# Turning half of a decoder's attention probabilities in 32 by 32 blocks on VectorE, with transfers within SBUF in place of TensorE transposes

## The chip, the cores and the metric

The kernel runs on one core of a Trainium2 chip. The metric is the device time of one execution in microseconds; a time of several runs is their median. TensorE, VectorE, ScalarE and GpSimd each work through their own instructions strictly in order, and so does SyncE, which here only issues transfers (DMA). An instruction that has to wait for another engine or for a transfer holds up everything behind it on its own engine. In views of the profile PE is TensorE, PEld its weight loads, DVE is VectorE, ACT is ScalarE, POOL is GpSimd, SP or SPq is SyncE.

## The reference

One decoder layer over 8 batch elements of 512 tokens with 256 channels, all in float32. Three blocks follow each other, each with a residual and a layer norm: a linear attention with its own MLP, a softmax cross-attention to a context of 512 tokens with 128 channels, and a feed-forward stage that picks one of 8 adapters for each batch element. The change touches the cross-attention alone, which is this:

```python
def _L0_xattn_ref(q, kv, Wq, Wk, Wv, Wo, bo):
    NUM_HEADS = 16
    HEAD_DIM = 64
    ...
    scores = jnp.einsum('bhnd,bhmd->bhnm', qh, kh) * scale
    attn = jax.nn.softmax(scores, axis=-1)
    out = jnp.einsum('bhnm,bhmd->bhnd', attn, vh)
    out = out.transpose(0, 2, 1, 3).reshape(B, N, INNER)
    return out @ Wo + bo
...
x = _layernorm(x + _L0_xattn_ref(x, ctx_512, ...), axis=-1)
```

There are 16 heads of 64 channels, 512 queries and 512 keys. For each batch element and head the probabilities are a 512 by 512 matrix.

## The kernel before

**How the work is cut.** A batch element's 512 tokens are NT = 4 chunks of 128. The cross-attention takes two heads together, a *pair*, so there are NPAIR = 8 pairs; one head's 64 channels lie on partitions 0 to 63 and the other's on 64 to 127. For each pair `cross_attention` projects queries, keys and values (`qT`, `kT`, `v2`), and then goes through two *halves* of two chunks each. For each chunk `soft` (from L764) does the following, with the two heads' work side by side:

1. TensorE makes the scores of 128 queries against 512 keys, for both heads, into one of two PSUM tiles of the room `sc` (L770).
2. VectorE takes the negated maximum over the keys (L777).
3. ScalarE takes the exponential into a tile `p`, one for each head, 128 queries on the partitions by 512 keys, and sums on the way (L785).
4. VectorE takes the reciprocal of the sums (L790).
5. GpSimd scales `p` by it (L796), or ScalarE does (L794).
6. TensorE turns `p` in four transposes of 128 by 128 into a PSUM bank (L806), since the weighing needs keys on the partitions.
7. ScalarE (L328), or VectorE (L330), copies the bank into the half's tile `pT` of that head.

When both chunks of a half have come so far, `weigh` multiplies `v2` by the two `pT` tiles in 16 matrix multiplications (L825), and the result is copied into `oT`. After each fourth pair `project_out` multiplies by `Wo` (L841). A `pT` tile holds 4 blocks of 128 keys by 256 queries; the columns of the result in `oT` are these 256 queries in order.

**Rooms.** Tiles come from named rooms with a fixed number of places. `p` has 8 places, `x` (a whole batch element's tokens) 5, `pT` 2 and two more that it shares with `prod`, the products of the linear attention (L515, L538). PSUM has 4 banks and 2 score tiles.

**What sets the order.** Nothing on the compute engines is ordered by hand. Each piece of work is given to `task` with its engine, its length in nanoseconds, a due time, what it reads and what it writes. Work with `others` can go to a second engine. `play` then steps through a model of time: whenever an engine is free, it takes the piece with the earliest due time whose inputs are ready and whose tiles have room. The instructions of each engine are written out in the order found, and that order is fixed from then on. A `slack` is added to the time at which a piece's results count as ready; for transfers it stands for the landing. Due times are in units of PACE = 3,200 ns, 64 of them for a batch element. The linear attention and the MLP of later batch elements, and the feed-forward stage of the one before, run between the pieces of the cross-attention.

**Transfers.** All are issued by SyncE: inputs and weights at the start, then for each batch element one load of `x` (L432), one of the context (L702), and one store of the result (L962; four for the last one, L956). Each transfer signals on one of 8 semaphores in turn.

Of the kernel before, what the change touches and what calls it, by code (L numbers as in the profile page):

```python
# [18 lines left out]
P = 128  # L19
B, S, C = 8, 512, 256  # L20
NT = S // P
# [8 lines left out]
NPAIR = H2 // 2  # L30
# [20 lines left out]
PACE = 3200.0  # L51

WINDOWS = {0: (-200, -136), 1: (-8, 34), 2: (34, 84), 3: (84, 136)}


@with_exitstack
def decoder(ctx: ExitStack, tc: tile.TileContext, t: dict, out: bass.AP):
# [29 lines left out]
    def room(name, n, shape, pool=const):  # L87
        rooms[name] = [[pool.tile(shape, F32, name=f"{name}_{i}"), 0.0] for i in range(n)]
# [90 lines left out]

    room("bank", 4, [P, 512], psum)  # L180
    room("sc", 2, [P, 2, S], psum)
    room("x", 5, [P, NT, C])
    room("xhat", 1, [P, NT, C])
    room("xnT", 1, [P, KC, S])
    room("y1", 1, [P, NT, C])
# [15 lines left out]
    room("qT", 1, [P, S])  # L201
    room("kT", 1, [P, S])
    room("v2", 2, [P, NT, P])
    room("p", 8, [P, S])

    room("pT", 2, [P, NT * 2 * P])
    rooms["pT"] += rooms["prod"][2:]
    room("oT", 5, [P, S])
    room("bu", 1, [P, C])
# [116 lines left out]
    def copy(e, dst, src):  # L326
        if e == "act":
            nc.scalar.copy(dst, src)  # L328
        else:
            nc.vector.tensor_copy(dst, src)  # L330
# [363 lines left out]
    def cross_attention(b, begin):  # L694
        x, x1T, ctx = xs[b], Val("x1T"), Val("ctx")
        P8 = 8 * PACE

        def when(pr, step):
            return begin + (8 * pr + step) * PACE

        task(
            "sp", 0, begin - 60000, lambda: nc.sync.dma_start(out=ctx.t, in_=t["ctxT"][b]), (), [(ctx, 0)], slack=4000  # L702
        )
        turn(x1T, x, when(0, -12))
        for c in range(NT):
            task(
                "pool", 730, when(0, 2 + c),
                lambda e, c=c: add(e, x.t[:, c, :], x.t[:, c, :], bo2),
                [(x, c)], [(x, c)], ("bo2",), others=[("dve", 420, 4000)],
            )  # L710
        goes = []
        out_norm = Norm(x)
        oTs = []
        for pr in range(NPAIR):
            cols = slice(pr * P, (pr + 1) * P)
            qT, kT, v2, oT = Val("qT"), Val("kT"), Val("v2"), Val("oT")
            oTs.append(oT)
            ps_q, ps_k, ps_v = Val("bank"), Val("bank"), Val("bank")

            def project_q(ps=ps_q, cols=cols):  # L720
                for kc in range(KC):
                    nc.tensor.matmul(ps.t, Wq[:, kc, cols], x1T.t[:, kc, :], start=kc == 0, stop=kc == KC - 1)  # L722

            def project_v(ps=ps_v, cols=cols):
                for m in range(NT):
                    keys = slice(m * P, (m + 1) * P)
                    nc.tensor.matmul(ps.t[:, keys], ctx.t[:, keys], Wv[:, 0, cols], start=True, stop=True)  # L727

            task("pe", mm(512, 2), when(pr, -9), project_q, chunks(x1T), [(ps_q, 0)], ("Wq",), "full", holds=[qT])
            task("act", 600, when(pr, -8.8), lambda ps=ps_q, qT=qT: nc.scalar.mul(qT.t, ps.t, D2**-0.5), [(ps_q, 0)], [(qT, 0)])  # L730
            task(
                "pe", mm(512, 1), when(pr, -8),
                lambda ps=ps_k, cols=cols: nc.tensor.matmul(ps.t, Wk[:, 0, cols], ctx.t, start=True, stop=True),
                [(ctx, 0)], [(ps_k, 0)], ("Wk",), "full", holds=[kT],
            )
            task(
                "act", 590, when(pr, -7.8), lambda e, ps=ps_k, kT=kT: copy(e, kT.t, ps.t), [(ps_k, 0)], [(kT, 0)],
                others=[("dve", 690, 1500)],
            )
            task("pe", mm(128, 4), when(pr, -3), project_v, [(ctx, 0)], [(ps_v, 0)], ("Wv",), "full", holds=[v2])  # L740
            task(
                "act", 600, when(pr, -2.5),
                lambda e, ps=ps_v, v2=v2: copy(e, v2.t.rearrange("p m d -> p (m d)"), ps.t), [(ps_v, 0)], [(v2, 0)],
                others=[("dve", 690, 1500)],
            )
            for half in range(2):
                pT = [Val("pT"), Val("pT")]
                for c in (2 * half, 2 * half + 1):
                    soft(qT, kT, pT, c, when(pr, 4 * half - 6) + 0.1 * (c % 2) * PACE, when(pr, 2 * c))
                weigh(v2, pT, oT, half, when(pr, 4 * half + 6))  # L750
            if pr % 4 == 3:
                for c in range(NT):
                    project_out(x, oTs[pr - 3 :], range(pr - 3, pr + 1), c, when(pr, (13, 15, 16, 17)[c]))
                    if pr == NPAIR - 1:
                        out_norm.stats(c, when(pr, 18))
        out_norm.scale(range(NT), when(NPAIR, 11))
        for c in range(NT):
            out_norm.put(x, c, when(NPAIR, 11) + c, "dve")

    def halves(pT):  # L760
        return pT.t[:, : NT * 2 * P].rearrange("p (m n) -> p m n", m=NT)


    def soft(qT, kT, pT, c, due, turn_due):  # L764
        ps, nmax, ssum, rinv = Val("sc"), Val("nmax"), Val("ssum"), Val("rinv")

        def scores():
            for i in range(2):
                rows = slice(i * D2, (i + 1) * D2)
                nc.tensor.matmul(  # L770
                    ps.t[:, i, :], qT.t[rows, c * P : (c + 1) * P], kT.t[rows, :], start=True, stop=True
                )

        task("pe", mm(512, 1), due, scores, [(qT, 0), (kT, 0)], [(ps, 0)], kind="rows")
        task(
            "dve", 1217, due + 0.2 * PACE,
            lambda: nc.vector.tensor_reduce(nmax.t, ps.t, AX.X, ALU.max, negate=True), [(ps, 0)], [(nmax, 0)],  # L777
        )
        ps_ = []
        for i in range(2):  # L780
            p = Val("p")
            ps_.append(p)
            task(
                "act", 788, due + (0.5 + 0.2 * i) * PACE,
                lambda i=i, p=p: nc.scalar.activation(  # L785
                    p.t, ps.t[:, i, :], AF.Exp, bias=nmax.t[:, i : i + 1], accum_out=ssum.t[:, i : i + 1]
                ),
                [(ps, 0), (nmax, 0)], [(p, 0), (ssum, i)], kind="exp",
            )
        task("dve", 158, due + 0.8 * PACE, lambda: nc.vector.reciprocal(rinv.t, ssum.t), [(ssum, 0), (ssum, 1)], [(rinv, 0)])  # L790
        for i, p in enumerate(ps_):
            def scale(e, i=i, p=p):
                if e == "act":
                    nc.scalar.mul(p.t, p.t, rinv.t[:, i : i + 1])  # L794
                else:
                    nc.gpsimd.tensor_scalar(p.t, p.t, rinv.t[:, i : i + 1], 1.0, ALU.mult, ALU.mult)  # L796

            task(
                "pool", 715, due + (1 + 0.2 * i) * PACE, scale, [(p, 0), (rinv, 0)], [(p, 0)],
                others=[("act", 631, 1200)],  # L800
            )
            bank = Val("bank")

            def transpose(p=p, bank=bank):
                for m in range(NT):
                    nc.tensor.transpose(bank.t[:, m * P : (m + 1) * P], p.t[:, m * P : (m + 1) * P], ident)  # L806

            task("pe", 436, turn_due + i * PACE, transpose, [(p, 0)], [(bank, 0)], kind="full", holds=[pT[i]])
            task(
                "act", 587, turn_due + (i + 0.2) * PACE,  # L810
                lambda e, i=i, bank=bank: copy(
                    e, halves(pT[i])[:, :, (c % 2) * P : (c % 2 + 1) * P], bank.t.rearrange("p (m n) -> p m n", m=NT)
                ),
                [(bank, 0)], [(pT[i], c % 2)], others=[("dve", 690, 1000)],
            )


    def weigh(v2, pT, oT, half, due):
        av = Val("bank")

        def emit():
            for m in range(NT):
                for i in range(2):
                    cols = slice(i * D2, (i + 1) * D2)
                    nc.tensor.matmul(  # L825
                        av.t[cols, : 2 * P], v2.t[:, m, cols], halves(pT[i])[:, m, :], start=m == 0, stop=m == NT - 1
                    )

        task("pe", 1728, due, emit, [(v2, 0)] + [(pT[i], j) for i in range(2) for j in range(2)], [(av, 0)], kind="cols", holds=[oT])
        def put(e):  # L830
            to, of = oT.t[:, half * 2 * P : (half + 1) * 2 * P], av.t[:, : 2 * P]
            copy(e, to, of)

        task("act", 370, due + 0.5 * PACE, put, [(av, 0)], [(oT, half)], others=[("dve", 424, 100)])
# [255 lines left out]
```

## Time and profile before

| | |
|---|---|
| Median of 3 runs | 1831.79 us (1829.74 to 1832.67) |
| Profiled execution, its own time | 1831.43 us |
| Its span, first to last instruction | 1829.7 us |
| Instructions | 24,550 |
| Mean granted TensorE clock | 0.969 |
| TensorE transposes of `p` (L806) | 2048, busy 291.5 us |
| Copies of the turned `p` on ScalarE | 404, 594 ns each |
| Copies of the turned `p` on VectorE | 108, 677 ns each |
| Transfers by SyncE, all sizes | 3.3% of 16 engines' span |

The profile is one execution. Its page gives the busy time of each engine, the span in 40 slices with a digit for each engine's busy tenths, and rows for groups of instructions: line, engine, operation, what it writes and reads, shapes and count, then busy microseconds and the mean nanoseconds of one, then the idle time of the engine just before them and whose end it waited for. A view of a stretch gives for each engine its busy time with the number of instructions, then the granted clock of TensorE, the share of the transfer engines, and GB/s. A view in order of time gives start, length, engine, line, operation and tiles. A view of transfers gives the count, the size of one and the median time from issue to landing. Matrix multiplications overlap each other, so the mean length of one is more than its share of TensorE's time; the distance from one start to the next is that share.

### The profile page before, as it was taken

The page shows a single profiled execution, that of the slowest core. Times are in us where ns is not written, and L with a number is a line of the kernel's source. Part 1 is how long each engine was busy: PE and PEld are TensorE (multiplying, and loading weights), DVE is VectorE, ACT ScalarE, POOL GpSimd, SP SyncE. Part 2 cuts the span into 40 slices and gives each one's busy share as a digit, 9 for nine tenths or more (in the row PEclk, how much of TensorE's full clock was granted, in tenths as well). Part 3 has the DMA queues.
Part 4 walks back from the last instruction along what each step waited for, and adds up shares of the span by engine and source line. Part 5 has one row for each costly group of instructions (what it writes and reads, how often), then busy time and mean ns, then how long its engine had stood idle before and what let it go on. Part 6 is the DMA issues. An engine that isn't in the chain of part 4 may idle for free.

```text
span 1829.7 us, 24550 instructions
## 1 busy us (share of the span) xinstructions
PE 1678.7 (92%) x8720; PEld 1025.2 (56%) x8720; DVE 1326.5 (72%) x2141; ACT 1117.0 (61%) x2423; POOL 1078.1 (59%) x913
## 2 busy tenths in 40 slices
PE   3638999999999989999999999999999999999996
PEld 1534556555656545665556655666556655665662
DVE  8998987887868787779758887769758444555444
ACT  0205756667756677667665776667666667556643
POOL 6557775787676764767537864588537321343432
PEclk7769999999999999999999999999999999999998
DMA  8000000000000000000000000000000000000000
GB/s 256 1 1 1 1 1 1 7 1 1 1 7 29 1 1 1 7 30 1 1 1 12 24 1 1 1 24 1 1 1 12 13 1 1 7 12 1 7 13 17
DMA packets 18458, 22.70 MB, mean 12 GB/s; under 512 B 2720, under 2 KB 15648, under 8 KB 18336
## 3 DMA queue, kind: packets, MB, share of 16 engines
q1 hardware_dynamic: 16928, 19.03, 3.3%
q0 software_dynamic: 1408, 2.10, 0.5%
q8 instruction: 69, 1.13, 0.3%
q14 instruction: 53, 0.43, 0.1%
HBM read 16.93 MB, written 4.19 MB: 12 GB/s over the span
## 4 chain that ended last, share of the span: by engine, by line
PE 59%; DVE 20%; POOL 4%; ACT 4%; issue 3%; DMA 0%; POOLq 0%; ACTq 0%; DVEq 0%
PE bank L825 10%; PE sc L770 9%; PE bank L806 9%; PE bank L841 5%; PE bank L618 4%; PE bank L722 4%; DVE nmax L777 4%; DVE kv L524 3%; PE bank L643 3%; DVE o L547 3%; PE bank L467 3%; PE bank L869 2%; PE bank L972 2%; PE bank L727 2%; ACT p L785 2%
## 5 line engine op out<-in xcount | busy, mean ns | idle before, releaser
L796 POOL TENSOR_SCALAR p<-p,rinv 128x512 f32<-128x512 f32 x392 | 280.5, 729 | 400.5 <-DVE rinv L790 335.5
L785 ACT ACTIVATE p<-sc,nmax 128x512 f32<-128x512 f32 x512 | 348.7, 689 | 142.4 <-DVE nmax L777 113.2
L777 DVE TENSOR_REDUCE nmax<-sc 128x2 f32<-128x1024 f32 x256 | 304.5, 1215 | 120.9 <-PE sc L770 120.3
L806 PEld LDWEIGHTS bank<-ident,p 128*128 128x128 f32 x2048 | 234.3, 141 | 160.0 <-issue 100.0
L806 PE MATMUL bank<-ident,p 128*128 128x128 f32 x2048 | 291.5, 276 | 15.5 <-ACT qT L730 4.1
L515 POOL TENSOR_TENSOR prod<-k,v 128x1088 f32<-128x1088 f32 x105 | 265.3, 2553 | 60.2 <-DVE k L493 41.1
L538 POOL TENSOR_TENSOR prod<-q,kv 128x1088 f32<-128x1088 f32 x93 | 248.4, 2688 | 63.1 <-DVE kv L524 28.8
L770 PE MATMUL sc<-kT,qT 64*128 64x512 f32 x1024 | 265.8, 626 | 8.4 <-ACT p L785 7.7
L524 DVE TENSOR_REDUCE kv<-prod 128x68 f32<-128x1088 f32 x128 | 162.5, 1276 | 22.9 <-POOL prod L515 22.7
L825 PE MATMUL bank<-pT,v 128*64 128x256 f32 x1056 | 163.1, 389 | 4.7 <-DVE y L599 2.3
L547 DVE TENSOR_REDUCE o<-prod 128x68 f32<-128x1088 f32 x128 | 160.6, 1272 | 9.1 <-POOL prod L538 8.8
L825 PE MATMUL bank<-prod,v 128*64 128x256 f32 x992 | 153.6, 385 | 4.1 <-ACT pT L328 1.3
L328 ACT COPY prod<-bank 128x512 f32<-128x512 f32 x196 | 111.1, 594 | 66.2 <-PE bank L806 65.0
L770 PEld LDWEIGHTS sc<-kT,qT 64*128 64x128 f32 x1024 | 87.5, 187 | 111.3 <-issue 82.7
L328 ACT COPY pT<-bank 128x512 f32<-128x512 f32 x208 | 119.9, 593 | 42.2 <-PE bank L806 41.7
L825 PEld LDWEIGHTS bank<-pT,v 128*64 128x64 f32 x1056 | 87.0, 138 | 64.9 <-issue 12.8
L643 PE MATMUL bank<-projT,h 128*128 128x256 f32 x512 | 119.5, 383 | 4.1 <-ACT h L679 2.7
L841 PE MATMUL bank<-Wo,oT 128*128 128x256 f32 x512 | 121.5, 381 | 1.7 <-ACT pT L328 1.7
L722 PE MATMUL bank<-x1T,Wq 128*128 128x512 f32 x256 | 122.3, 600 | 0.8 <-DVE x1T L330 0.4
L982 DVE SCALAR_TENSOR_TENSOR h<-bank,decb,xT 128x512 f32<-128x512 f32 x128 | 89.2, 742 | 36.8 <-PE bank L972 36.5
L841 PEld LDWEIGHTS bank<-Wo,oT 128*128 128x128 f32 x512 | 94.8, 190 | 29.7 <-issue 12.7
L643 PEld LDWEIGHTS bank<-projT,h 128*128 128x128 f32 x512 | 93.8, 190 | 26.3 <-issue 8.7
(138 smaller groups left out, 2824.8 us busy)
## 6 DMA issues: line engine op xcount, KB each, us to landing
x<-in_x SPq DMA_DIRECT2D x7, 512.0 KB, 3.9
out<-x SPq DMA_DIRECT2D x7, 512.0 KB, 2.9
ctx<-in_ctxT SPq DMA_DIRECT2D x8, 256.0 KB, 2.6
fcT<-in_fcT SPq DMA_DIRECT2D x1, 1024.0 KB
projT<-in_projT SPq DMA_DIRECT2D x1, 1024.0 KB
Wq<-in_Wq SPq DMA_DIRECT2D x1, 1024.0 KB, 10.4
Wo<-in_Wo SPq DMA_DIRECT2D x1, 1024.0 KB, 13.2
x<-in_x SPq DMA_DIRECT2D x4, 128.0 KB, 2.3
```

Source lines behind the costliest of these rows:

```text
L328: nc.scalar.copy(dst, src)
L515: (nc.gpsimd if e == "pool" else nc.vector).tensor_tensor(pr.t.rearrange("p (d e h) -> p d e h", d=DSPLIT, h=H1), k.t[:, s : s + DSPLIT, : ...
L524: nc.vector.tensor_reduce(kv.t[:, :, s : s + DSPLIT].rearrange("p e d -> p d e"), pr.t.rearrange("p (d e h) -> p d e h", d=DSPLIT, h=H1), ...
L538: (nc.gpsimd if e == "pool" else nc.vector).tensor_tensor(pr.t.rearrange("p (h e d) -> p h e d", h=DSPLIT, d=D1), q.t[:, s : s + DSPLIT, : ...
L643: nc.tensor.matmul(ps.t[:, :C], of(f, c), projT[:, f, :], start=f == fs[0], stop=f == fs[-1])
L770: nc.tensor.matmul(ps.t[:, i, :], qT.t[rows, c * P : (c + 1) * P], kT.t[rows, :], start=True, stop=True)
L777: lambda: nc.vector.tensor_reduce(nmax.t, ps.t, AX.X, ALU.max, negate=True), [(ps, 0)], [(nmax, 0)],
L785: lambda i=i, p=p: nc.scalar.activation(p.t, ps.t[:, i, :], AF.Exp, bias=nmax.t[:, i : i + 1], accum_out=ssum.t[:, i : i + 1]),
L796: nc.gpsimd.tensor_scalar(p.t, p.t, rinv.t[:, i : i + 1], 1.0, ALU.mult, ALU.mult)
L806: nc.tensor.transpose(bank.t[:, m * P : (m + 1) * P], p.t[:, m * P : (m + 1) * P], ident)
L825: nc.tensor.matmul(av.t[cols, : 2 * P], v2.t[:, m, cols], halves(pT[i])[:, m, :], start=m == 0, stop=m == NT - 1)
L841: nc.tensor.matmul(ps.t[:, :C], oT.t[:, c * P : (c + 1) * P], Wo[:, pr, :], start=pr == prs[0], stop=pr == prs[-1])
```

## The change

For the second half of every pair of batch elements 1 to 7 (`BLOCKED`), step 6 and 7 are replaced. VectorE turns `p` in 32 by 32 blocks, straight into a tile `blk` in SBUF. In `blk` the partition is a key's place within its block of 32, but still in the group of 32 partitions in which the query lay; so `place` lets SyncE issue 16 transfers for each head, each of 32 partitions with 4 runs of 64 elements (256 bytes), which put every block at its keys' partitions in `pT`. The queries of the half then lie in another order in `pT` and so in the PSUM result of `weigh`, and the copy into `oT` puts them back. `blk` gets a room of two tiles, 4 KB on each partition; `x` goes from 5 to 4 places and `p` from 8 to 6. Batch element 0 and all first halves stay as they were.

```diff
+BLOCKED = {b: [(pr, 1) for pr in range(NPAIR)] for b in range(1, B)}
...
-    room("x", 5, [P, NT, C])
+    room("x", 4, [P, NT, C])
...
-    room("p", 8, [P, S])
+    room("p", 6, [P, S])
...
+    room("blk", 2, [P, 16, 2, 32])
...
                 pT = [Val("pT"), Val("pT")]
+                blk = [Val("blk"), Val("blk")] if (pr, half) in BLOCKED.get(b, ()) else None
                 for c in (2 * half, 2 * half + 1):
-                    soft(qT, kT, pT, c, when(pr, 4 * half - 6) + 0.1 * (c % 2) * PACE, when(pr, 2 * c))
-                weigh(v2, pT, oT, half, when(pr, 4 * half + 6))
+                    soft(qT, kT, pT, blk, c, when(pr, 4 * half - 6) + 0.1 * (c % 2) * PACE, when(pr, 2 * c))
+                if blk:
+                    for i in range(2):
+                        place(pT[i], blk[i], when(pr, 4 * half + i))
+                weigh(v2, pT, oT, half, bool(blk), when(pr, 4 * half + 6))
...
+            if blk:
+
+                task(
+                    "dve", 610, turn_due - (3 - i) * PACE,
+                    lambda i=i, p=p: nc.vector.transpose(blk[i].t[:, :, c % 2, :], p.t),
+                    [(p, 0)], [(blk[i], c % 2)],
+                )
+                continue
             bank = Val("bank")
...
+    def place(pT, blk, due):
+
+
+        def emit():
+            for j in range(4):
+                for g in range(4):
+                    nc.sync.dma_start(
+                        out=halves(pT)[32 * j : 32 * j + 32, :, 64 * g : 64 * g + 64],
+                        in_=blk.t[32 * g : 32 * g + 32, j::4, :, :].rearrange("k m c n -> k m (c n)"),
+                    )
+
+        task("sp", 4600, due, emit, [(blk, c) for c in range(2)], [(pT, c) for c in range(2)], slack=2500)
...
+            if blocked:
+                to = to.rearrange("p (c g n) -> p g c n", c=2, g=4)
+                of = of.rearrange("p (g c n) -> p g c n", c=2, g=4)
             copy(e, to, of)
```

In the changed kernel the lines are shifted: the scores are L777, the maximum L784, the exponential L792, the reciprocal L797, the scaling L803 or L801, the block transpose L813, the transposes of TensorE L821, the copies L331 and L333, the transfers of `place` L838, and the weighing L853.

More of the change, by code (lines that the diff above doesn't have):

```diff
@@ L761, in halves, with soft @@
         return pT.t[:, : NT * 2 * P].rearrange("p (m n) -> p m n", m=NT)
-    def soft(qT, kT, pT, c, due, turn_due):
+    def soft(qT, kT, pT, blk, c, due, turn_due):
         ps, nmax, ssum, rinv = Val("sc"), Val("nmax"), Val("ssum"), Val("rinv")
@@ L815, in soft, with weigh @@
             )
-    def weigh(v2, pT, oT, half, due):
+    def place(pT, blk, due):
[7 more added lines that the diff above has]
+        task("sp", 4600, due, emit, [(blk, c) for c in range(2)], [(pT, c) for c in range(2)], slack=2500)
+    def weigh(v2, pT, oT, half, blocked, due):
         av = Val("bank")
```

## The prediction

> **What bounds the kernel now.** I read the page's busy shares first, then the slices, then one stretch without the start and the end, then the rows of the work that the change touches, and last SyncE's queue in order of time, since the change puts 1,792 transfers on it.
>
> ```profile
> PE 1678.7 (92%) x8720; PEld 1025.2 (56%) x8720; DVE 1326.5 (72%) x2141; ACT 1117.0 (61%) x2423; POOL 1078.1 (59%) x913
> ...
> PE   3638999999999989999999999999999999999996
> ...
> DVE  8998987887868787779758887769758444555444
> ...
> PEclk7769999999999999999999999999999999999998
> ```
>
> ```profile
> 200.00:1760.00 1560.00, 1511.77 (x8005) 920.05 (x8003) 1117.85 (x1824) 1036.07 (x2239) 931.29 (x788) 1.00 0.02 6
> ```
>
> TensorE is the bound. Between 200 and 1760 us it is busy 1511.77 of 1560 us (97%) at full clock; VectorE, the second number after PEld, has 1117.85 us (72%). DMA is at 0.02 of its engines. So a microsecond taken off TensorE is worth nearly a microsecond there, and a wait put onto its queue costs nearly one.
>
> ```profile
> L796 POOL TENSOR_SCALAR p<-p,rinv 128x512 f32<-128x512 f32 x392 | 280.5, 729 | 400.5 <-DVE rinv L790 335.5
> ...
> L806 PE MATMUL bank<-ident,p 128*128 128x128 f32 x2048 | 291.5, 276 | 15.5 <-ACT qT L730 4.1
> ...
> L328 ACT COPY pT<-bank 128x512 f32<-128x512 f32 x208 | 119.9, 593 | 42.2 <-PE bank L806 41.7
> ```
>
> ```profile
> 1104.74 0.60 PE L806 MATMUL bank<-ident,p 128*128 128x128 f32 x4
> 1105.17 1.89 PE L643 MATMUL bank<-projT,h 128*128 128x256 f32 x8
> ```
>
> L806 is what goes: four transposes occupy TensorE from 1104.74 to 1105.17, 0.43 us to the next start; 291.5 us over 512 such groups is 0.57.
>
> ```profile
> 3.53 0.43 SPq L263 DMA_DIRECT2D wqkv<-in_wqT  x1
> 4.00 0.47 SPq L266 DMA_DIRECT2D bqkv<-in_bq  x1
> 4.52 0.43 SPq L263 DMA_DIRECT2D wqkv<-in_wkT  x1
> ```
>
> ```profile
> out<-x SPq DMA_DIRECT2D x7, 512.0 KB, 2.9
> ...
> ctx<-in_ctxT SPq DMA_DIRECT2D x8, 256.0 KB, 2.6
> ...
> out<-x SPq DMA_DIRECT2D x4, 128.0 KB, 1.7
> ```
>
> These are the prices of the new path. One after another, SyncE's transfers start every 0.47 to 0.52 us, whatever they carry; standing alone, with the queue rested, one takes 0.33 to 0.40. From issue to landing a small one needs 1.7 us.
>
> **Removed from TensorE.** 7 batches x 8 pairs = 56 halves, each with 2 chunks x 2 heads = 224 tiles, 896 of 2048 transposes. At 0.43 to 0.57 a group: 96 to 128 us. I take 0.50: **-112**, nearly all of it on the path at 97% busy.
>
> **Removed copies.** The order of the changed kernel has 214 PSUM copies into pT and prod on ScalarE and 69 on VectorE, where there were 404 and 108. ScalarE loses 190 x 0.593 = 113 us, and is not the bound: 0.
>
> **VectorE.** Added: 224 transposes of 128x512. No such row exists. Bounds: its copy of 128x512 from PSUM took 0.676, and a product with both inputs in SBUF beside GpSimd took 2.251 for 1088 columns, 1.06 for 512; below, its copy of half as much, 128x256, at 0.420. I take 0.68, the nearest row: 152 us, less 39 copies x 0.68 = 27 gone, net +125 (67 to 211). Its share in the stretch rises from 72 to 80%, so most is covered by its own idle time; where it is fullest (790 of 1000 us from 200 to 1200) scores wait behind it in line. I take a tenth, **+12** (0 to 60).
>
> The Trainium skill, VectorE: DVE Perf Modes, section "The three transpose paths", gives 311 ns for 128x128 of a two-byte type on VectorE; four of them would make 1.24 us a tile, an estimate, and 278 us instead of 152. No row here shows it.
>
> **SyncE's transfers.** place() issues 16 transfers of 32 KB for each head of a half, 32 for a half. At 0.475 from start to start, one head takes 7.6 us of queue, both 15.2, and the last lands 1.7 later: 16.9 us from the first issue. Queue load is 56 x 15.2 = 851 us in some 1,400: it isn't full. But the diff's own costs for the planner are 4,600 ns and 2,500 of slack, 11.7 us for both heads, and the order on every engine is written out by those. So the data come 5.2 us later than the order reckons, 56 times: 291 us if nothing covered it, 0 if all is covered. Two places can expose it.
>
> First, TensorE's weighing (L853). I counted, in the changed order, the TensorE work between the scores of a half's second chunk and that half's weighing, priced by the timeline's start-to-start (0.45 for four transposes, 0.88 for a chunk's scores, 1.78 for a weighing): 11 to 47 us, median 35. The chain that must fit: scores to reciprocal (pairing the k-th with the k-th: median 5.6 us, quartiles 4.4 and 7.8), scaling 0.73, two block transposes 1.4 behind one maximum of 1.2, then 16.9: 25.8, or 28.0 at the upper quartile. Nine halves have less than 25.8, together 25 us short; 13 have less than 28, 48 short; at 32 it is 119. I take **+45**, since TensorE's waits feed on (0 to 119).
>
> Second, VectorE: 110 of the 224 block transposes wait for landings, because the blk room has one tile per head. Behind such a wait stand the maxima (L784), reciprocals and sums that ScalarE and then TensorE need. VectorE idles 442 us in the stretch, 7.9 a pair, so 5.2 can be lost without a trace or reach TensorE whole. p's room goes from 8 tiles to 6, which shortens the run-ahead that would hide it. Between 0 and 291 minus the first place's 45, I take 1 us a pair, **+56**.
>
> The rows also say how the queue may be held up: out and x transfers stand in line with place(), and the trace shows an out waiting up to 188 us at the head of SyncE's queue. The order puts seven of them between places; I count that within the range.
>
> The trace speaks against one worry. A transfer reuses one of 8 semaphores and so waits for the eighth before it; eight issues take 3.8 us, and 1.7 to 2.9 is less. The Trainium skill, DMA: Bandwidth & Descriptors, section "Rules for kernel authors", says to coalesce small transfers, since under 64 KB most of the time is overhead. Its roughly 2 us of fixed cost, paid one after another by 1,792 transfers, would be 3,600 us, an estimate; rows 0.47 us apart show that issue overlaps landing, so only the direction of the rule holds.
>
> **Waits.** Each weighing waits for 8 semaphores for each head instead of one or two: some 8 more waiting instructions x 0.051 us (an EVENT_SEMAPHORE on L806) x 56 = 23 us at most on TensorE, 0 if its sequencer runs ahead. **+11**.
>
> **Clock.** From 0 to 200 us TensorE is busy 58% at 0.79 of full clock; above 95% it is 0.99 to 1.00. With waits of some us in it, it may lose a little: **+5** (0 to 30).
>
> The reordered copy of oT moves the same elements: 0. x's room going from 5 to 4 is covered: loads land in 3.9 us, a batch takes 205.
>
> **Sum.** Profiled execution 1831.4 (span 1829.7), the median of the three runs is 1831.8. 1831.4 - 112 + 12 + 45 + 56 + 11 + 5 = 1848.4. **Forecast 1848, slower by 0.9%**; it holds as a case while the two exposures together cost 89 to 153 us, so its own range is 1836 to 1900.
>
> **Rivals.** *The transfers come in time.* If back-to-back SBUF transfers issue like the rested ones, 0.37 apart, a half takes 11.8 + 1.7 = 13.5, 1.8 late instead of 5.2. The two places shrink to a third: 1831.4 - 112 + 12 + 15 + 19 + 11 + 5 = 1781. For it: out took 0.38 alone; against: every stretch of back-to-back issues shows 0.47 and more, tiny loads too.
>
> *SyncE becomes the bound.* One mechanism: landing under load gets longer than eight issues take (3.8 us), and each transfer then waits for its semaphore. The load burst at the start shows 5 to 13 us to landing. At 6, a head takes 2 x 6 = 12 us, a half 24 + 6 = 30, 18.3 late, and 24 is the pace of a pair itself (205 / 8 = 25.6). With the two places at 3.5 times: 1831.4 - 112 + 12 + 158 + 196 + 16 = 2101; at 4.5 us to landing, 9 a head, 18 + 4.5 = 22.5 a half and 10.8 late: 1831.4 - 112 + 12 + 93 + 116 + 16 = 1956. It decides from 3.8 us on. Against it: that burst moved 250 GB/s, while 16 x 32 KB in 7.6 us is 69.
>
> *It does nothing to TensorE's bound* because another engine fills the hole: ScalarE and GpSimd are at 66 and 60% in the stretch; no.
>
> **How the numbers follow.** Late data give back the gain and more, 1848: 0.50. In time, 1781: 0.33. SyncE the bound, above 1900: 0.12. The remaining 0.05 is an even balance. Resolution is about 0.2% (3.7 us): faster 0.36, same 0.06, slower 0.58. Cases of both signs hold much of the chance, so the range goes from 1770, below the first rival, to 1940, just short of the second.
>
> **What would show it.** Right: place transfers 0.45 to 0.5 us apart on SyncE; TensorE busy near 1,560; new idle time before L853 released by DMA, some tens of us, and VectorE idle before L813 with a DMA as releaser; L813 near 0.68. Wrong: 0.37 apart and no DMA among TensorE's releasers; or transfers waiting for each other on SyncE; or L813 above 1 us, with VectorE full.

## The result, and the profile after

| | before | after |
|---|---|---|
| Median of 4 runs each, side by side | 1832.23 us | 2130.03 us (2127.35 to 2133.84) |
| Ratio after to before | | 1.163 (95%: 1.1607 to 1.1652) |
| Span of the profiled execution | 1829.7 us | 2129.5 us |
| TensorE busy / idle in that span | 1678.7 / 151.0 us | 1691.9 / 437.6 us |
| Mean granted TensorE clock | 0.969 | 0.897 |

The kernel is 16.3% slower. The direction was forecast, the size was not: 1848 with a range up to 1940.

First the page of the changed kernel: busy time of each engine, the slices, and the chain that ended last.

```profile
PE 1691.9 (79%) x7824; PEld 981.1 (46%) x7824; DVE 1448.9 (68%) x2319; ACT 1035.4 (49%) x2255; POOL 1052.5 (49%) x903
...
PE   3568998889877888887878779786998888886856
...
DVE  8979969778876857586476867677685444553424
...
PEclk7779999899988999898899989998999998998978
...
PE 34%; SPq 29%; DVE 20%; DMA 5%; issue 5%; ACT 3%; POOL 1%; DVEq 0%; POOLq 0%; ACTq 0%
```

Two things are to be seen. TensorE has 896 matrix transposes fewer (7824 instructions instead of 8720), and yet its busy time is 13 us longer. And its idle time has nearly trebled. No engine is full now: the row of nines in TensorE's slices is gone, nothing else has one, and SyncE's issuing (SPq) has 29% of the chain where it had no part; the chain of before was:

```profile
PE 59%; DVE 20%; POOL 4%; ACT 4%; issue 3%; DMA 0%; POOLq 0%; ACTq 0%; DVEq 0%
```

The same stretch as before, without start and end, has a lower clock too (before it was 1.00):

```profile
200.00:2060.00 1860.00, 1536.97 (x7201) 887.09 (x7199) 1248.09 (x2028) 964.00 (x2092) 916.25 (x786) 0.91 0.15 37
```

The 0.15 is the share of the 16 transfer engines: they are far from full. What is late is the issuing. The line of `place` in the view of one source line gives count, then shortest, median and longest duration of an issue in ns, and under it who waited for these transfers (us, times):

```profile
L838 SPq DMA_DIRECT2D pT<-blk x1232: 353/599/1900, 381.1 to 2069.1; - x176
L838 SPq DMA_DIRECT2D prod<-blk x560: 585/599/1786, 557.2 to 2041.8; - x187
...
  DVE blk L813: 280.3, 58
  PEld bank L853: 118.2, 19
  PE bank L853: 117.0, 21
```

SyncE in order of time, the two heads of one half (start, length, then the count of transfers):

```profile
1021.83 11.56 SPq L838 DMA_DIRECT2D pT<-blk  x16
1033.50 10.24 SPq L838 DMA_DIRECT2D prod<-blk  x16
```

From start to start the median is 0.644 us, so a head takes 16 x 0.644 = 10.3 us of queue, a half 20.6, and with 1.9 us to landing (the median for 32 KB in e1 and in e3 below) 22.5 us. The order on the engines reckons with 11.7. The data are 10.8 us late, not 5.2.

Who pays is in the list of waits (engine, line, what it waited for, then us in all, times, longest):

```profile
DVE blk L813 <- DMA prod<-blk: 141.8, 26, 9.4
DVE blk L813 <- DMA pT<-blk: 138.5, 32, 9.3
ACT p L792 <- DVE blk L813: 126.0, 34, 9.5
...
PE bank L853 <- DMA prod<-blk: 67.3, 10, 9.4
...
PE bank L853 <- DMA pT<-blk: 49.7, 11, 9.6
```

These are the two places that the prediction named. TensorE stands at the weighing for 117 us. VectorE stands at the block transpose for 280 us, because `blk` isn't free before its last transfer has landed, and ScalarE's exponentials stand 126 us behind block transposes, for want of a place in `p`, which the waiting transposes still hold. SyncE, too, stood: 485.6 us at `place`, until the block transposes had filled `blk`. So its queue wasn't full. In the rows, the new transpose itself is as cheap as forecast, 701 ns:

```profile
L813 DVE STREAM_TRANSPOSE blk<-p 128x512 f32<-128x512 f32 x224 | 154.8, 701 | 311.6 <-DMA prod<-blk 141.8
...
L853 PE MATMUL bank<-pT,v 128*64 128x256 f32 x1096 | 250.8, 430 | 70.7 <-DMA pT<-blk 49.7
...
L853 PE MATMUL bank<-prod,v 128*64 128x256 f32 x952 | 215.0, 412 | 68.7 <-DMA prod<-blk 67.3
```

**Where TensorE's busy time went.** One such wait, TensorE in order of time, and the same microseconds as stretches (length, busy time of PE, PEld, DVE, ACT, POOL, then the granted clock):

```profile
1232.54 0.65 PE L853 MATMUL bank<-pT,v 128*64 128x256 f32 x2
1242.60 0.66 PE L853 MATMUL bank<-prod,v 128*64 128x256 f32 x1 [9.42 <-DMA prod<-blk]
...
1243.06 0.63 PE L853 MATMUL bank<-prod,v 128*64 128x256 f32 x1
...
1243.48 0.63 PE L853 MATMUL bank<-prod,v 128*64 128x256 f32 x1
```

```profile
1231.00:1233.00 2.00, 2.00 (x10) 0.58 (x6) 1.17 (x3) 0.00 (x0) 1.87 (x3) 1.00 0.22 53
1233.00:1235.00 2.00, 0.18 (x1) 0.00 (x0) 1.05 (x1) 0.00 (x0) 0.87 (x1) 1.00 0.21 49
1235.00:1236.00 1.00, 0.00 (x0) 0.00 (x0) 0.00 (x0) 0.00 (x0) 1.00 (x1) 0.72 0.15 36
1236.00:1242.00 6.00, 0.00 (x0) 0.00 (x0) 0.00 (x0) 0.00 (x0) 0.58 (x1) 0.50 0.23 54
1242.00:1245.00 3.00, 2.40 (x12) 1.60 (x13) 2.42 (x3) 0.50 (x1) 0.00 (x0) 0.50 0.00 0
1245.00:1246.00 1.00, 1.00 (x6) 0.27 (x2) 1.00 (x2) 0.28 (x2) 0.00 (x0) 0.66 0.00 0
1246.00:1248.00 2.00, 2.00 (x11) 1.74 (x11) 0.92 (x4) 1.93 (x6) 0.58 (x1) 1.00 0.07 16
```

The weighing began with the first head's data and stood 9.42 us for the second's. Some two us after the last multiplication had ended, the clock fell to 0.50, and it stayed there for three us after the work had come back: one head's multiplications start 0.43 us apart (1243.06, 1243.48), where those of a weighing that didn't wait start 0.21 apart (1020.35, 1020.57 and 1020.78 in the same trace). So such a wait is paid twice, and the second part is booked as busy time. Not every wait is: of the 38 idle stretches of TensorE over 3 us after the first 200 us, 30 had a fall of the clock, four began at half clock already, and four of 3.7 to 4.1 us passed without a fall. I worked this part out for whole traces, from stretches of one microsecond after the first 200: busy time times what the clock lacked to 1.00. It is 9.4 us before, in 6 falls of the clock, and 104.3 us after, in 50 falls. The mean clock of the runs of before lay between 0.963 and 0.971, and their times between 1829 and 1836 us, so differences of a few us in this part say nothing.

With that, the 299.8 us between the two spans are: idle +286.6; lost to the clock +94.9; the rest of TensorE's busy time, which is what the removed transposes gave, -81.7. It is this split that the experiments below are read by.

### The profile page after: what moved, and what is told of

Read it like the earlier page. It is cut to its first block, busy times and chain, and to the rows that moved or that the text cites. A ratio compares the mean times of both kernels' runs of the same rounds, so it can differ in the third digit from the quotient of the medians.

```text
span 2129.5 us, 25289 instructions
## 1 busy us (share of the span) xinstructions
PE 1691.9 (79%) x7824; PEld 981.1 (46%) x7824; DVE 1448.9 (68%) x2319; ACT 1035.4 (49%) x2255; POOL 1052.5 (49%) x903
## 3 DMA queue, kind: packets, MB, share of 16 engines
q1 hardware_dynamic: 274976, 77.87, 14.4%
## 4 chain that ended last, share of the span: by engine, by line
PE 34%; SPq 29%; DVE 20%; DMA 5%; issue 5%; ACT 3%; POOL 1%; DVEq 0%; POOLq 0%; ACTq 0%
SPq L838 29%; PE bank L853 8%; PE sc L777 5%; DVE o L550 3%; PE bank L821 3%; PE bank L872 3%; DVE kv L527 3%; DVE nmax L784 2%; PE bank L621 2%; DVE prod L541 2%; DMA pT<-blk 2%; DMA prod<-blk 2%; PE bank L470 2%; PE bank L646 2%; ACT p L792 2%
## 5 line engine op out<-in xcount | busy, mean ns | idle before, releaser
L803 POOL TENSOR_SCALAR p<-p,rinv 128x512 f32<-128x512 f32 x383 | 279.0, 741 | 620.7 <-DVE rinv L797 576.3
L792 ACT ACTIVATE p<-sc,nmax 128x512 f32<-128x512 f32 x512 | 348.7, 689 | 307.4 <-DVE nmax L784 144.5
L813 DVE STREAM_TRANSPOSE blk<-p 128x512 f32<-128x512 f32 x224 | 154.8, 701 | 311.6 <-DMA prod<-blk 141.8
L784 DVE TENSOR_REDUCE nmax<-sc 128x2 f32<-128x1024 f32 x256 | 304.0, 1214 | 79.7 <-PE sc L777 77.5
L518 POOL TENSOR_TENSOR prod<-k,v 128x1088 f32<-128x1088 f32 x100 | 253.0, 2547 | 113.9 <-DVE k L496 59.3
L853 PE MATMUL bank<-pT,v 128*64 128x256 f32 x1096 | 250.8, 430 | 70.7 <-DMA pT<-blk 49.7
L777 PE MATMUL sc<-kT,qT 64*128 64x512 f32 x1024 | 275.8, 642 | 13.0 <-ACT p L792 12.9
L853 PE MATMUL bank<-prod,v 128*64 128x256 f32 x952 | 215.0, 412 | 68.7 <-DMA prod<-blk 67.3
L821 PE MATMUL bank<-ident,p 128*128 128x128 f32 x1152 | 174.4, 287 | 60.0 <-ACT qT L733 23.6
L821 PEld LDWEIGHTS bank<-ident,p 128*128 128x128 f32 x1152 | 135.1, 146 | 172.1 <-issue 112.3
L853 PEld LDWEIGHTS bank<-pT,v 128*64 128x64 f32 x1096 | 126.5, 152 | 155.9 <-issue 79.5
L527 DVE TENSOR_REDUCE kv<-prod 128x68 f32<-128x1088 f32 x128 | 161.0, 1272 | 11.8 <-POOL prod L518 11.7
L853 PEld LDWEIGHTS bank<-prod,v 128*64 128x64 f32 x952 | 110.1, 146 | 113.5 <-issue 70.3
L331 ACT COPY oT<-bank 128x256 f32<-128x256 f32 x113 | 42.2, 374 | 231.5 <-PE bank L853 231.2
L777 PEld LDWEIGHTS sc<-kT,qT 64*128 64x128 f32 x1024 | 92.2, 194 | 119.9 <-issue 77.9
L470 PE MATMUL bank<-wqkv,xnT 128*128 128x512 f32 (+1 forms) x256 | 101.0, 531 | 19.1 <-DVE x L879 11.7
```

The lines of the kernel that those rows point to most:

```text
L518: (nc.gpsimd if e == "pool" else nc.vector).tensor_tensor(pr.t.rearrange("p (d e h) -> p d e h", d=DSPLIT, h=H1), k.t[:, s : s + DSPLIT, : ...
L527: nc.vector.tensor_reduce(kv.t[:, :, s : s + DSPLIT].rearrange("p e d -> p d e"), pr.t.rearrange("p (d e h) -> p d e h", d=DSPLIT, h=H1), ...
L777: nc.tensor.matmul(ps.t[:, i, :], qT.t[rows, c * P : (c + 1) * P], kT.t[rows, :], start=True, stop=True)
L792: lambda i=i, p=p: nc.scalar.activation(p.t, ps.t[:, i, :], AF.Exp, bias=nmax.t[:, i : i + 1], accum_out=ssum.t[:, i : i + 1]),
L853: nc.tensor.matmul(av.t[cols, : 2 * P], v2.t[:, m, cols], halves(pT[i])[:, m, :], start=m == 0, stop=m == NT - 1)
```

## The experiments

**e1, the price of an issue alone.** A kernel with nothing but groups of transfers, one group after another on SyncE: within SBUF in several shapes, from HBM, and to HBM.

```diff
+    for i in range(N):
+        nc.sync.dma_start(out=runs(d1, 32 * (i % 4), 32, 4, 64, 512 * (i // 4)), in_=runs(src, 32 * (i // 4), 32, 4, 64, 512 * (i % 4)))
...
+    for i in range(N):
+        nc.sync.dma_start(out=d3[:32, 1024 + 64 * i : 1024 + 64 * i + 64], in_=flat[32 * i : 32 * i + 32, :64])
```

> Leaves the whole decoder out: groups of transfers issued back to back by SyncE, 16 of a kind, to price one issue. In the changed kernel one 32x4x64 transfer within SBUF held SyncE 0.599 us, where the loads of before held it 0.433. Theory 'source and target': any transfer within SBUF costs about 0.60, whatever its shape, and loads and stores 0.43. Rival 'runs': the price follows the number of runs (128 runs of 256 bytes, two levels on both sides), so 32x256 in one run each and 32x64 come at 0.43 or less, 32x8x64 near 0.8, and a load or store of 32x4x64 at 0.60 too. Rival 'few partitions': everything on 32 partitions costs 0.60, everything on 128 costs 0.43. The same transfer issued by ScalarE: 0.60 by the first, unknown by the others.

One line for each group, from the view of its source line; the durations are shortest, median and longest, in ns. L39 is the transfer of the changed kernel, 32 partitions with 4 runs of 64 elements within SBUF. L41 is 32 partitions with one run of 256 elements within SBUF, L43 32 with one run of 64, L45 128 with one of 64, L47 32 with 8 runs of 64, L49 128 with 4 runs (128 KB); L51 loads 128 partitions with one run of 64 from HBM, L53 loads 32 partitions with one run of 64 from HBM, L55 32 with 4 runs; L62 stores 32 with 4 runs.

```profile
L39 SPq DMA_DIRECT2D d<-src x16: 585/600/757, 5.2 to 17.6; - x16
L41 SPq DMA_DIRECT2D d<-src x16: 588/589/597, 18.2 to 27.7; - x16
L43 SPq DMA_DIRECT2D d<-src x16: 588/589/597, 28.4 to 37.9; - x16
L45 SPq DMA_DIRECT2D d<-src x16: 592/599/607, 38.5 to 48.2; - x16
L47 SPq DMA_DIRECT2D d<-src x16: 586/610/681, 48.8 to 59.2; - x16
L49 SPq DMA_DIRECT2D d<-src x8: 643/659/703, 59.8 to 64.7; - x8
L51 SPq DMA_DIRECT2D d<-in_x x16: 423/598/672, 65.5 to 74.5; - x16
L53 SPq DMA_DIRECT2D d<-in_x x16: 414/419/428, 75.2 to 82.1; - x16
L55 SPq DMA_DIRECT2D d<-in_x x16: 422/430/431, 82.6 to 89.7; - x16
L62 SPq DMA_DIRECT2D out<-src x16: 430/430/449, 98.0 to 105.1; - x16
```

Up to 64 KB the shape hardly matters: one run of 64 elements (8 KB) takes 0.589 us and eight (64 KB) 0.610; 128 KB take 0.659, in part beside ScalarE's issues. What matters is where from and where to: within SBUF 0.59 to 0.61 us, from or to HBM 0.42 to 0.45, with L51 as the exception. There ScalarE was issuing 16 transfers of L39's kind at the same time, at 0.613 us each in the median. The rivals (number of runs, few partitions) fall. The trace of before held only the second kind, since no transfer there stayed within SBUF.

**e2, half of the transfers.** 8 of 16 for each head; half of each `pT` tile isn't written.

```diff
-            for j in range(4):
+            for j in range(2):
                 for g in range(4):
```

> place() issues 8 of its 16 transfers, so half of each blocked pT keeps what lay there before; all else, the order on every engine too, is that of the changed kernel. Theory 'issue time': a head takes 8 x 0.644 = 5.2 us of SyncE instead of 10.3, close to the 4.6 that the order reckons with, and the data come some 1 us late instead of 12 to 13; the time falls by some 330 to 380 us to 1750 to 1800, below the kernel before. Rival 'not the issue': block transposes of 0.70 us, more waits for each instruction and the lower clock set the time, which stays above 2000.

One run: 1790.66 us against 1833.28 before. A half now takes 2 x 5.2 + 1.9 = 12.3 us, nearly what the order reckons, and the waits for the data are nearly gone (the second number counts them):

```profile
  DVE blk L813: 13.0, 10
  PE bank L853: 7.4, 2
```

The rest of the change is in place, so the slowness lies in the transfers; that it is their lateness, and not their number, e3 shows for most of it. Of the 124 weighings that ran without a wait and at full clock, 104 take the same 1.57 us from first to last start as those of before. The other 20 take up to 0.44 us longer, 5.2 us together.

**e3, the same transfers, reckoned honestly.** Only the times that the order is made with are changed. The 2,500 of slack stayed, where the expectation says 2,000.

```diff
-                    "dve", 610, turn_due - (3 - i) * PACE,
+                    "dve", 705, turn_due - (3 - i) * PACE,
...
-        task("sp", 4600, due, emit, [(blk, c) for c in range(2)], [(pT, c) for c in range(2)], slack=2500)
+        task("sp", 10400, due, emit, [(blk, c) for c in range(2)], [(pT, c) for c in range(2)], slack=2500)
```

> The same transfers, but the order is written out with their measured price: 10,400 ns of SyncE and 2,000 of slack for a head, 705 ns for a block transpose. Theory 'late against the order': the data are as slow as before, but nothing is placed in front of them that has to wait, so most of the loss goes: 1820 to 1900. Rival 'SyncE is full': 20.6 us of queue for each half cannot go into a pair of 24 to 26 us, so the time stays above 2000, whatever the order.

One run: 1875.65 us. With the same 1,792 transfers at the same price, some 254 of the 298 us are back; VectorE waits 63.9 us for data and TensorE 37.5, where it was 280.3 and 117.0:

```profile
  DVE blk L813: 63.9, 29
  PE bank L853: 37.5, 11
...
DMA to landing us min/median/max: 1.9/1.9/3.6
```

So most of the loss isn't the queue's work as such, but an order written out for data that come 10.8 us later than it says. It still stays above before: the waits for data that are left are a quarter to a third of what they were, and the rooms (e4) and the block transposes (e7) have their own price.

**e4 and e6, the smaller rooms alone.** The kernel before, with fewer places.

```diff
-    room("x", 5, [P, NT, C])
+    room("x", 4, [P, NT, C])
...
-    room("p", 8, [P, S])
+    room("p", 6, [P, S])
```

> The kernel before with x at 4 and p at 6 places alone. If the rooms are covered, as the prediction had it: 1832, within 4 us. If they cost run-ahead by themselves: 1840 to 1860.

Both: 1853.8 us, ratio 1.0118 (1.0101 to 1.0135), so +20 to +22 us, where the prediction had put `x` at nothing and only named `p`. It isn't waiting for a place alone: the planner also shared the work out anew, and VectorE is busy 1397.6 us instead of 1326.5.

> The kernel before with p at 6 places and x left at 5. Both rooms together cost 20 us. Theory 'run-ahead': the softmax of the next chunks can't start while six probability tiles wait, so it is p: 1848 to 1855. Rival: it is x, since a batch element's load then waits for a store: 1832 to 1836.

Only `p` at 6: 1842.31 us, ratio 1.0046 (1.0029 to 1.0063), between the two expectations. `p` costs about half of it, 8 to 10 us; that `x` costs the other half follows by difference only, and was not run alone.

**e7, the block transposes alone.** As e4, with the 224 block transposes on VectorE beside TensorE's own, and nothing transferred.

```diff
+            if blk:
+                task(
+                    "dve", 705, turn_due - (3 - i) * PACE,
+                    lambda i=i, p=p: nc.vector.transpose(blk[i].t[:, :, c % 2, :], p.t),
+                    [(p, 0)], [(blk[i], c % 2)],
+                )
             bank = Val("bank")
```

> The kernel before with x at 4 and p at 6 places, and the 224 block transposes on VectorE beside TensorE's own; their result is not used, nothing is transferred. Against the 1854 of these rooms alone. Theory of the prediction: a tenth of their 157 us shows, 1865 to 1875. Rival 'hidden': 1850 to 1858. Rival 'VectorE is close to being a bound': half of it or more, 1930 and up.

1865.27 us, ratio 1.0178 (1.0161 to 1.0195): +11.5 over e4.

```profile
L807 DVE STREAM_TRANSPOSE blk<-p 128x512 f32<-128x512 f32 x224 | 152.2, 695 | 32.3 <-POOL p L798 29.6
```

152.2 us of added work on VectorE cost a thirteenth of themselves. VectorE is busy only 97 us longer than in e4, since the order gave other pieces to ScalarE and GpSimd.

**e8, the price that was forecast.** 12 of 16 transfers make a head take 12 x 0.644 = 7.7 us, which is the 7.6 of the prediction, and the data 2 x 7.7 + 1.9 - 11.7 = 5.6 us late, where it had 5.2. A quarter of `pT` isn't written.

```diff
-            for j in range(4):
+            for j in range(3):
                 for g in range(4):
```

> place() issues 12 of its 16 transfers, so a quarter of each blocked pT keeps what lay there before; the rest is the changed kernel. 12 x 0.644 = 7.7 us of SyncE for a head: the 7.6 that the prediction took for 16. So this is the prediction's sum put to the test at its own price. If only the price of an issue was wrong: 1848; with the rooms, which alone cost 20 where 0 was taken: 1868, and up to 1890 if TensorE's clock falls further than was reckoned. Rival 'the exposures are mis-sized too': above 1910.

1910.4 us (1907.22 to 1923.81), ratio 1.0451 (1.0408 to 1.0494): above the 1848 and the range up to 1890, and at the edge of the rival's "above 1910", which the time alone can't refuse. The page's first line and the waits for data:

```profile
PE 1642.6 (86%) x7824; PEld 960.7 (50%) x7824; DVE 1446.6 (76%) x2319; ACT 1033.9 (54%) x2255; POOL 1052.1 (55%) x903
```

```profile
DVE blk L813 <- DMA pT<-blk: 48.4, 18, 6.3
DVE blk L813 <- DMA prod<-blk: 36.7, 12, 7.5
PE bank L853 <- DMA prod<-blk: 20.7, 9, 3.8
PE bank L853 <- DMA pT<-blk: 20.6, 4, 7.3
```

TensorE's multiplications wait 41.3 us for data, where the prediction took 45. Its idle time in all is 1905.6 - 1642.6 = 263.0, which is 112 more than before, where the prediction's idle terms make 12 + 45 + 56 + 11 = 124. Of the 112, 12 are the rooms' (e4), so 100 stand against 124: the exposures were not too small for the price that was assumed, and the rival's reason falls. What is missing to 1910 is not idle time: TensorE's busy time fell by 36 and not by 107 (112 gained, 5 given back to the clock). 45 us went to the clock in 28 falls (54.4 against 9.4), and the transposes gave 81.

**e5 and e9, one transfer for both heads.** The tiles of both heads are made one (`blk` and a new room `pB`, each with one tile for two heads), so that a transfer carries 64 KB in 8 runs and a half needs 16 instead of 32. The order reckons 10,700 ns and 2,100 of slack.

```diff
-    room("blk", 2, [P, 16, 2, 32])
-    rooms["pT"] += rooms["prod"][2:]
+    room("pB", 1, [P, 2, NT * 2 * P])
+    room("blk", 1, [P, 2, 16, 2, 32])
+    rooms["pT"] = rooms["prod"][2:]
...
-                        out=halves(pT)[32 * j : 32 * j + 32, :, 64 * g : 64 * g + 64],
-                        in_=blk.t[32 * g : 32 * g + 32, j::4, :, :].rearrange("k m c n -> k m (c n)"),
+                        out=pT.t.rearrange("p i (m n) -> p (i m) n", m=NT)[32 * j : 32 * j + 32, :, 64 * g : 64 * g + 64],
+                        in_=blk.t[32 * g : 32 * g + 32, :, j::4, :, :].rearrange("k i m c n -> k (i m) (c n)"),
```

> One transfer carries both heads (32 partitions, 8 runs of 64): 16 transfers for a half instead of 32, with the same bytes and the same 256-byte runs, and the order reckons with 10,700 ns and 2,100 of slack for them. Theory 'number of issues': a half takes 16 x 0.65 = 10.5 us of SyncE and its data are there 12.6 us after the first issue, 10 us sooner than in the honest order; the time is 1770 to 1800, below before. Rival 'bytes or runs in flight': landing grows with twice the runs in each transfer and eats that up: 1840 to 1880, as with the honest order.

1821.48 us (1817.76 to 1823.17), ratio 0.9943 (0.9927 to 0.996). The issue costs no more with twice the bytes, as e1 had it, and the waits for data are small; but the time stands between the two expectations. The table below says why: the gain is 91 and not 112, the clock takes 27, and of the 50 us of idle time 22 are there without any transfer (e7).

```profile
L837 SPq DMA_DIRECT2D pB<-blk x896: 585/609/1934, 389.6 to 1755.4; - x180
...
  PE bank L855: 12.4, 2
  DVE blk L812: 8.8, 8
```

This agrees with the direction of the Trainium skill, DMA: Bandwidth & Descriptors, section "Rules for kernel authors", to put small transfers together; what it saves here is 896 issues of 0.6 us on SyncE's queue. Against e3, which has twice the issues and is reckoned honestly too, the time falls by 54 us; the rooms for the tiles differ as well.

e9 changes one thing in e5: the block transposes fall due three units of PACE earlier, so that transfers start earlier.

```diff
-                    "dve", 705, turn_due - (3 - i) * PACE,
+                    "dve", 705, turn_due - (6 - i) * PACE,
```

> One transfer for both heads as in e5, and the block transposes due 3 PACE (9.6 us) sooner, so that VectorE takes them ahead of more of the linear attention's sums. Theory 'the rest of the loss is waiting and the lower clock that comes with it': the data are there sooner, TensorE waits less, 1780 to 1805. Rival 'VectorE's queue': what is taken out of line holds up maxima and sums, 1820 to 1850.

1788.74 us (1787.25 to 1790.05), ratio 0.9764 (0.9748 to 0.9781): 2.4% faster than before, and the fastest of all the kernels that leave nothing out. It forms the same probabilities by the same block transposes; it carries them in half as many transfers, in an order that leaves time for them.

**All traces by one split.** Each column is the difference to the trace of before in us: idle time of TensorE (span less busy time), what the clock took (worked out as above), and the rest of its busy time.

| Kernel | idle | clock | rest | mean clock |
|---|---|---|---|---|
| after | +286.6 | +94.9 | -81.7 | 0.897 |
| e8, 12 of 16 transfers | +112.0 | +45.0 | -81.1 | 0.942 |
| e3, honest order | +90.9 | +33.1 | -79.8 | 0.940 |
| e5, merged | +49.9 | +26.9 | -90.8 | 0.946 |
| e9, merged, earlier | +33.9 | +14.5 | -92.2 | 0.959 |
| e2, 8 of 16 | +28.9 | +17.1 | -86.8 | 0.956 |
| e7, rooms and block transposes | +21.6 | +8.0 | +3.3 | 0.966 |
| e4, rooms | +12.4 | +8.5 | +0.4 | 0.965 |
| e6, `p` alone | -0.2 | +11.5 | -0.2 | 0.962 |

The rest is near zero in the three kernels that keep all of TensorE's transposes, and 80 to 92 in the six that leave out 896 of them. That is what leaving them out was worth. In e6 the whole +11 stands under the clock, at a difference of 4 falls; of the clock's +8 to +12 in e4, e6 and e7 no more can be said.

## Why the prediction was wrong in size

**The step that failed: the price of an issue.** "At 0.475 from start to start, one head takes 7.6 us of queue." It was read from loads out of HBM, and of those from the first rows. From 6.97 us on the same burst has issues of 0.38 to 3.63 us, so "every 0.47 to 0.52 us, whatever they carry" was not so even there:

```profile
20.21 3.63 SPq L244 DMA_DIRECT2D enc<-in_enc  x1
```

Within SBUF the issue takes 0.60 us and 0.644 from start to start (e1 and the trace after), 10.3 us a head, so the data come 10.8 us late instead of 5.2. The nearest row was of another kind of transfer, and the highest price that the text named was 0.52. From e8, which has the forecast price, to the changed kernel it is 1910.4 to 2130.0: 220 of the 282 us by which the forecast missed.

**The exposure** (+45 at the weighing, +56 at the block transposes, +12 and +11). The places were right, and so was the size of the first at the assumed price: in e8 TensorE waits 41.3 us for data at the weighing. The rest of e8's idle time, without the rooms' 12, is some 58 us against 79. It doesn't grow in proportion: 1.9 times the lateness gave 2.6 times the idle time (286.6). The reason given, that waits feed on, fits ScalarE's 126 us behind waiting block transposes, but no run isolates it.

**The clock** (+5, 0 to 30): +94.9, and +45 in e8. The prediction counted waits as time lost once. The trace shows the second part: half clock for some us after most of the long ones. This is the larger part of the 59 us by which e8's profiled execution (1907.4) lies above 1848.4: 40 from the clock and 31 from the gain, less 12 from the idle time.

**The gain** (-112, 96 to 128): -80 to -92. It lies below even the bound that goes by 0.43 us a group (96). The 20 slower weighings of e2 (5.2 us) are a small part of the difference. Why the transposes were worth less than their distance from one start to the next is open otherwise.

**VectorE** (+12): right, e7 shows 11.5; 701 ns each against 680, and not the 1,240 that the prediction worked out beside it. **Semaphores** (+11): at most the 5.2 us of e2's slower weighings. **ScalarE's copies** (0): ScalarE is busy 82 us less; that nothing came of it was not run alone. The trace has 219 of these copies where the prediction counted 214. **Rooms** (0 for `x`, and `p` only named): +20 to 22, wrong; "loads land in 3.9 us, a batch takes 205" looked at the transfer and not at how long the batch's tile is held, though that this is the reason was not shown.

**The rivals.** In time (1781): fell, no issue within SBUF took 0.37 in a row. Its sum was a fair one for data that come nearly in time: e2, 0.6 us late, took 1790.7. SyncE the bound: its mechanism fell, since landing takes 1.9 us (e3), no issue of `place` is seen to wait for another transfer, and SyncE itself waited 485.6 us for block transposes. But the lateness that it worked with, 10.8 us, is what came, by another cause, and even so its 1956 was 174 short, from the clock and the faster than proportional idle time.

**Open.** Why an issue within SBUF takes 0.17 us more is not shown by any run. That the falls of the clock follow the waits is read from the trace, microsecond by microsecond, and no run takes the one away without the other. A second tile of `blk` for each head might hide much of VectorE's 280 us; this was not run.

## What to carry to other kernels

When a change issues many transfers in a row, count issues times their price, by kind of transfer, before counting bytes; the row for loads doesn't hold for transfers within SBUF, and measuring a dozen of them alone takes one short kernel. Where an order is written out from reckoned times, a transfer reckoned too short is paid for far from its own queue: from e8 to the changed kernel 5.2 us more lateness in each of 56 halves, 291 us in all, cost 220. Correcting the reckoning alone gave back 254 us (e3), where the work that was moved was worth 80 to 92. Halving the issues, with the rooms that this needs, gave 54 more (e5), and an earlier due time 33 (e9). A wait of several us on TensorE can cost more than the wait: a fall of the clock took 2.1 us on average (104.3 us in 50 falls), and between 1.6 and 2.8 in the other nine traces.

## What the runs showed of the hardware

- An issue on SyncE takes 0.59 to 0.61 us within SBUF whatever the shape from 8 to 64 KB, and 0.42 to 0.45 from or to HBM, one after another with SyncE alone issuing (e1). In the one group of loads during which ScalarE issued transfers too, an issue on SyncE took 0.598 us in the median and 0.423 at the least. That group was also the only one of loads to 128 partitions in e1; but the first loads to 128 partitions in the trace of before took 0.43 to 0.47, so the shape alone doesn't explain it. It is one group, and no run isolates it.
- At the wait shown, TensorE's clock halved some 2.2 us after the last end (1233.19; mean of 0.72 from 1235 to 1236) and came back 3.1 us after the work (1242.60; 0.66 from 1245 to 1246). It is no fixed delay: in the idle stretches over 3 us of the same trace the fall came 1.4 to 5.3 us after the last end, and full clock 2.9 to 14.4 us after the restart. By the trace's clock records each time at half clock lasted 3.41 us or 2 to 5 times that, but for the last, which the end of the trace cuts. The Trainium skill, TensorE: Matmul & The Clock Gate, section "Part 1: The HAM clock gate", has the clock halved after an idle window and restored after a busy one, of about 3.4 us each. The halving and the 3.41 us agree. In this kernel, which waits often, it took 104.3 of 2129.5 us, 4.9%.
